# Making the last block's cross keys, first values, first norm and first queries inside its self-attention, and running both cross stages' value matmuls one step later

## The chip, the cores and the metric

The kernel runs on one core of one Trainium2 chip. A core has a matmul engine (PE, whose weight loads the profile calls PEld), a vector engine (DVE), a scalar engine (ACT), GpSimd (POOL) and DMA queues (SP issues most of them). Each engine takes its instructions in the order in which the program gives them; between engines there are semaphores. The metric is the device time of one execution in microseconds; three runs of the kernel took 4175.94 to 4178.57, median 4177.94.

## The reference, cut to what matters

`x` is 4 sequences of 512 tokens of width 256, `ctx` 4 sequences of 64 tokens of width 192, all float32. Four blocks follow each other: block 0 is cross attention with a feed-forward, block 1 self-attention, cross attention and a gated feed-forward, block 2 four layers of a state-space scan, and block 3:

```python
h = _layernorm(x, ln1_g, ln1_b)
x = x + _mha(h, h, sa_wq, sa_bq, ...)           # 16 heads of 16
h = _layernorm(x, ln2_g, ln2_b)
x = x + _mha(h, context, ca_wq, ca_bq, ...)     # keys and values from ctx
h = _layernorm(x, ln3_g, ln3_b)
h = gelu(h @ mlp_w1.T + mlp_b1) @ mlp_w2.T + mlp_b2
return x + h
```

## The kernel before, in words

A sequence of 512 tokens is four tiles of 128 tokens; there are 16 tiles (NT). `X` holds the residual of all 16 tiles in SBUF.

`layer3` (block 3, line 1784) loads its weights, runs `self_stage`, then `cross_kv`, then `cross_stage`. `layer0` (line 1115 on) runs `cross_kv` and the same `cross_stage`. In both stages the order of the instructions is written out by hand (`tc.manual_schedule()`). Pieces of work are kept in `Pieces`: a piece is a matmul function, an eviction function and a condition. `work(n)` takes the first piece whose condition holds from the queues `front`, `prep`, `fill`, in this order (and at most one from `fill` per call), and issues its matmuls; `evict(n)` issues the evictions of what `work` issued and then n steps of the generator at the head of `norms`. `until(ok)` alternates the two until a condition holds.

`self_stage` (line 849) loops over 64 softmax steps `k` in block 3 (`SPG` = 16 for each of 4 sequences) and four more. A step issues scores (L948, two PSUM tiles of two banks), the maximum nm (DVE, L959), four exponentials (ACT, L963), the transposes of the step before (PE, L977), whose copies pT are made by ACT (L980) and DVE (L982), and the values' matmuls (L996). Between them stand projections of the next sequence (ps_q, ps_k, ps_v; L185 is the helper `matmul_k`), the norm of the next sequence (`norm`, L612 to L622, with rstd on POOL in L616 and a bias added to X on POOL in L1112) and the output projection ps_wo with its eviction into X (L917). All projections share one PSUM buffer, "mi". After the last sequence the four ps_wo stand alone.

`cross_kv` (line 227 on) makes the cross keys and values: two key groups (ps_k), whose eviction kT_c (L249) DVE spreads over the heads with a mask into the block-diagonal Kbd (L250), Vbd zeroed on POOL (L233) and four value groups ps_v, evicted in two halves each (L271).

`cross_stage` (line 654) first makes the norm of sequence 0 (block 3 only), its transposes (`features`, ps_tr, L639, evicted as hT in L646) and two query groups (ps_q, evicted as qT in L678). Its loop then runs over 19 steps i: scores of tile i (L761, one PSUM buffer), nm and pr (DVE, L770, L772), the exponential (ACT, L773), transposes of tile i-2 (L792) with copies on ACT (L793), the sums and reciprocal of tile i (L778, L779), the division on POOL (L781), and at every odd i from 3 on the values' matmuls of the tile pair (i-3)/2 (L801), with a copy AT on ACT (L810). The output projections of that pair (ps_wo, added to X in L708) go to `front`. When a sequence's four tiles are in X, the second norm (xf), its transposes and hF follow, and `half(b)` issues the feed-forward's first half, 8 groups ps_f (GELU in L731), at i = 8 and 12 and twice behind the loop; it waits for its features with `until`. The second half, ps_w (L747, then a DMA to the output), is `fill` work for later steps. In block 0 `side` work of block 2's prefix runs in between.

Of the kernel before, what the change touches and what calls it, by code (L numbers as in the profile page):

```python
# [8 lines left out]
F32 = mybir.dt.float32  # L9
AF = mybir.ActivationFunctionType  # L10
ALU = mybir.AluOpType
AX = mybir.AxisListType
PSUM = bass.MemoryType.PSUM
DRAM = bass.MemoryType.DRAM

P = 128
B = 4
T = 512
# [39 lines left out]
class Pieces:  # L58
# [47 lines left out]
    def until(self, ok):  # L106
        for _ in range(200):
            if ok():
                return
            self.evict()  # L110
            if not ok():
                self.work()
        raise RuntimeError("a piece never comes")
# [11 lines left out]
def kernel(ctx: ExitStack, tc: tile.TileContext, t: dict, out: bass.AP):  # L125
# [15 lines left out]
    def col(name, i=0, n=1):  # L141
        at = _COL[name][0] + i
        return cols[:, at : at + n]
# [507 lines left out]

        return mm, ev, lambda: b in xns

    def cross_stage(X, pool, psum, Kbd, Vbd, Wq, bq, Wo, W1, b1, W2, ln_q, ln_f, bias_q, bias_f, store=None, side=None, g_tiles=None):

# [7 lines left out]
        if side:  # L665
            side(todo.besides, psum, ("mi", 3))
        at = {"wo": 0, "ff": 0}

        def project(b, c):
            def mm():  # L670
# [12 lines left out]
        def queries(b):  # L683
            if ln_q is None:
                xns[b] = X[:, b * TPB : (b + 1) * TPB, :]
            todo.prep.extend(features(pool, psum, xns, hTs, b, c, ln_q) for c in range(DC))
            todo.prep.extend(project(b, c) for c in range(DC))
# [123 lines left out]
            todo.front.extend(out(g, jj) for jj in range(2))  # L811

        with tc.manual_schedule():
            if ln_q is not None:
                for _ in norm(pool, X, 0, xns, bias_q):
                    pass
            queries(0)
            for i in range(NT + 3):
                b, j = divmod(i, TPB)
                if i < NT and j == 0:  # L820
                    if b >= 2:
                        half(b - 2)
                    if b < B - 1:
                        if ln_q is not None:
                            todo.norms.append(norm(pool, X, b + 1, xns, bias_q))
                        queries(b + 1)
                todo.evict(0)
                if i < NT:
                    scores(i)
                todo.work(2)  # L830
                todo.work_aside()
                todo.go_on(1)
                if 0 <= i - 2 < NT:
                    transposes(i - 2)
                todo.evict(3)
                if i < NT:
                    divided(i)
                todo.work(2, 0)
                if i >= 3 and i % 2 == 1:
                    through_values((i - 3) // 2)  # L840
            for b in (B - 2, B - 1):
                half(b)
            todo.until(lambda: at["ff"] == B)
            while todo.aside or todo.pend:
                todo.work_aside()
                todo.evict(0)
            assert todo.empty()

    def self_stage(X, pool, psum, wide, project, values, Wo, ln, bias, at_end=None, side=None):

# [186 lines left out]
        with tc.manual_schedule():  # L1039
            for _ in norm(pool, X, 0, xns, bias):  # L1040
                pass
            begin(0)
            K = NG * SPG
            lead = 4 if wide else 2
            for k in range(K + 4):
                n, r = divmod(k, SPG)
                if k < K and r == 0:
                    if n < NG - 1:
                        begin(n + 1)
                    elif at_end:  # L1050
                        prep.append((lambda: None, lambda ps: at_end(), None))
                    if n % G == 0 and n // G < B - 1:
                        norms.append(norm(pool, X, n // G + 1, xns, bias, lag=6 if side else 1))
                evict()
                back = k and k <= K
                if back:
                    transposes(k - 1, 0)
                todo.work_aside()
                if k < K:
                    scores(k)  # L1060
                    softmaxed(k)
                if back and k % spc == 0:
                    rs = sums[k // spc - 1]
                    nc.vector.reciprocal(rs, rs)
                if wide:
                    work()
                    evict(0)
                todo.go_on(1)
                through_values(lead // 2)
                evict(0)  # L1070
                if k % 2 or not todo.busy:
                    todo.go_on(1)
                todo.work_aside()
                work()
                evict()
                if back:
                    transposes(k - 1, 1)
                todo.go_on(1)
                todo.work_aside()
                through_values(lead // 2)  # L1080
                evict(0)
                work()
                if back and (wide or (k - 1) % 2 == 1):
                    c, r1 = divmod(k - 1, spc)
                    hc = 2 * c + combos(k - 1)[0][0] // 2
                    pv.extend((hc, t4) for t4 in range(TPB))
            until(lambda: at["wo"] == NG)
            while todo.side or todo.aside or todo.pend:
                todo.work_aside()
                evict()  # L1090
                todo.go_on(1)
            assert todo.empty() and not pv
# [688 lines left out]
                assert not active and len(banks) == 2  # L1781


    def layer3(X, wa):
        with ExitStack() as st:
            wp = st.enter_context(tc.tile_pool(name="w3", bufs=1))
            Wcq = load_w(wp, "L3_cq", [P, DC, D])
            Wck = load_w(wp, "L3_ck", [CP, 2, D], CP)
            Wcv = load_w(wp, "L3_cv", [CP, 2, D], CP)
            Wco = load_w(wp, "L3_co", [P, DC, D])  # L1790
            W1 = load_w(wp, "L3_w1", [P, DC, FF])
            W2 = load_w(wp, "L3_w2", [P, FF // P, D])
            bv, bo, cbv, cbo, mb2 = (row(wp, n) for n in ("l3_bv", "l3_bo", "l3_cbv", "l3_cbo", "l3_mb2"))
            with tc.tile_pool(name="a3s", bufs=1) as pool, tc.tile_pool(name="ps3s", bufs=1, space=PSUM) as psum:

                V2 = [pool.tile([P, TPB, T], F32, name=f"V{i}") for i in range(2)]
                for v in V2:
                    nc.gpsimd.memset(v, 0.0)

                def project(ps, k, m, hT, to=None):  # L1800
                    if hT is not None:
                        matmul_k(ps, [(wa["qk"[k]][:, c, m * P : (m + 1) * P], hT[:, c, :]) for c in range(DC)])
                    elif k == 0:
                        nc.vector.tensor_scalar(to, ps, col("l3_bq", m), 0.25, ALU.add, ALU.mult)
                    else:
                        nc.vector.tensor_scalar(to, ps, col("l3_bk", m), None, ALU.add)  # L1806

                def values(ps, n, j, hT, V=None):
                    if hT is not None:
                        matmul_k(ps[:, :D], [(hT[:, c, j * P : (j + 1) * P], wa["v"][:, c, :]) for c in range(DC)])  # L1810
                        return None
                    V = V2[n % 2]
                    nc.vector.tensor_add(
                        V.rearrange("p c (h r) -> p c h r", r=32)[:, j, :, :16],
                        ps[:, :D].rearrange("p (h r) -> p h r", r=16),
                        bv.rearrange("p (h r) -> p h r", r=16),
                    )
                    return V

                self_stage(X, pool, psum, False, project, values, wa["o"], ("l3_g1", "l3_b1"), bo)  # L1820
            with tc.tile_pool(name="a3c", bufs=1) as pool:
                with tc.tile_pool(name="ps3k", bufs=2, space=PSUM) as psum:
                    Kbd, Vbd = cross_kv(pool, psum, Wck, Wcv, 16, "l3_cbk", cbv)

                def store(i, x):
                    nc.sync.dma_start(out=out[i // TPB, (i % TPB) * P : (i % TPB + 1) * P, :], in_=x)

                with tc.tile_pool(name="ps3c", bufs=1, space=PSUM) as psum:
                    cross_stage(
                        X, pool, psum, Kbd, Vbd, Wcq, "l3_cbq", Wco, W1, "l3_mb1", W2,  # L1830
                        ("l3_g2", "l3_b2"), ("l3_g3", "l3_b3"), cbo, mb2, store,
                    )

    hT_pool = ctx.enter_context(tc.tile_pool(name="hT_pool", bufs=1))
# [46 lines left out]
    with ExitStack() as st:  # L1881
# [13 lines left out]
                nc.sync.dma_start(out=wa[n], in_=t[f"L3_{n}"].rearrange("(c p) n -> p c n", p=P))  # L1895

        layer2(hT, A, far[:, 0:1], h63, tail, X, fw, wl, late)
        layer3(X, wa)


# [68 lines left out]
```

## Time and profile before

| | |
|---|---|
| three runs | 4175.94 to 4178.57 us, median 4177.94 |
| the profiled execution | 4180.51 us, its span 4178.4 us, mean granted clock 0.905 |
| busy share of the span | PE 84%, DVE 72%, POOL 57%, ACT 53% |
| block 0's cross stage, first scores to last ps_w | 26.3 to 277 us |
| block 3's self-attention, last softmax step's nm to last ps_wo | 3899.2 to 3919.5 us |
| block 3's cross keys and values, norm and queries | 3919.5 to 3941 us |
| block 3's first cross scores to the last ps_w | 3941.1 to 4175.4 us |

The profile is one execution. "Busy" is the time in which an engine executes; behind a row of a timeline or of the groups stands in brackets how long the engine sat idle ahead of it and who released it. In a timeline a row is a run of equal instructions: start, length, engine, line, operation, tiles, number. Each float32 matmul of the program shows as two instructions (x8 is four matmuls). The granted clock is a share of PE's full clock.

### The profile page before, as it was taken

What the parts mean: (1) busy time and instruction counts of PE and PEld (TensorE: products, weight loads), DVE (VectorE), ACT (ScalarE), POOL (GpSimd) and SP (SyncE); (2) the same over time, 40 slices, a digit from 0 to 9 for tenths busy, and PEclk for the clock granted to TensorE, in tenths of its full rate; (3) what the DMA queues carried; (4) which work ended last, traced back from release to release, by engine and by line L of the source; (5) the groups of instructions that cost most, each with busy time, mean ns of one, the idle gap of its engine ahead of it and who ended that gap; (6) DMA issues with size and microseconds to landing.
All of it is one profiled execution on the core that took longest, in us unless ns stands there. A gap on an engine that the chain in (4) does not pass through costs nothing. (4 is left out here: it accounts for less than half of the span.)

```text
span 4178.4 us, 48642 instructions
## 1 busy us (share of the span) xinstructions
PE 3494.9 (84%) x17616; PEld 2186.1 (52%) x17616; DVE 3000.8 (72%) x2857; ACT 2195.9 (53%) x4457; POOL 2364.5 (57%) x1601
## 2 busy tenths in 40 slices
PE   7988988988888898788877787888877667999789
PEld 4654544544566464555555555555555444555446
DVE  5537456465555633999999999999999996666653
ACT  2345465454312434666666666666666553566322
POOL 2239259077100413989888988999988881000131
PEclk9999999999988997888888888888888778999899
DMA  2023023033100202444444444444443441000000
GB/s 75 5 86 104 27 74 98 18 91 97 44 1 1 66 18 83 160 152 158 149 162 145 157 154 160 153 153 147 161 157 132 147 144 36 1 1 1 1 6 16
DMA packets 140287, 369.93 MB, mean 89 GB/s; under 512 B 20624, under 2 KB 38224, under 8 KB 140048
## 3 DMA queue, kind: packets, MB, share of 16 engines
q1 hardware_dynamic: 136688, 363.58, 25.6%
q10 hardware_dynamic: 3360, 3.25, 0.3%
q8 instruction: 139, 2.28, 0.2%
q14 instruction: 100, 0.82, 0.1%
HBM read 363.50 MB, written 3.28 MB: 88 GB/s over the span
## 5 line engine op out<-in xcount | busy, mean ns | idle before, releaser
L1617 POOL TENSOR_TENSOR dBu<-dtx,bB 128x1022 f32<-128x1022 f32 x512 | 1198.7, 2361 | 49.1 <-DVE ps_dA L1644 36.8
L1644 DVE TENSOR_TENSOR_SCAN ps_dA<-ps_dA,dBu 128x1024 f32<-128x1024 f32 x384 | 877.9, 2286 | 129.6 <-POOL dBu L1617 88.8
L1629 ACT ACTIVATE ps_dA<-dt,A 128x512 f32<-128x512 f32 x1024 | 708.3, 692 | 469.9 <-DVE hC L1651 426.3
L1677 PE MATMUL ps_y<-ident,hC 128*128 128x128 f32 x3072 | 460.0, 303 | 51.3 <-DVE hC L1651 51.1
L1651 DVE TENSOR_TENSOR hC<-ps_dA,bC 128x1024 f32<-128x1024 f32 x384 | 469.8, 1223 | 23.9 <-issue 0.4
L1677 PEld LDWEIGHTS ps_y<-ident,hC 128*128 128x128 f32 x3072 | 406.8, 158 | 149.5 <-DVE hC L1651 75.6
L963 ACT ACTIVATE pr<-ps_s,nm 128x512 f32<-128x512 f32 x512 | 345.2, 686 | 257.5 <-DVE nm L959 257.5
L959 DVE TENSOR_REDUCE nm<-ps_s 128x2 f32<-128x1024 f32 x256 | 301.5, 1219 | 173.2 <-PE ps_s L948 156.4
L1655 POOL TENSOR_TENSOR hP<-hP,bC 128x1024 f32<-128x1024 f32 x128 | 301.9, 2358 | 108.4 <-issue 36.2
L977 PE MATMUL ps_pt<-ident,pr 128*128 128x128 f32 x2048 | 285.2, 279 | 65.3 <-DVE pT L982 39.5
L977 PEld LDWEIGHTS ps_pt<-ident,pr 128*128 128x128 f32 x2048 | 232.7, 142 | 164.5 <-issue 65.1
L1644 DVE TENSOR_TENSOR_SCAN hP<-ps_dA,dBu 128x1024 f32<-128x1024 f32 x128 | 291.7, 2279 | 0.0
L616 POOL TENSOR_TENSOR ln_rstd<-ln_rstd,const 128x4 f32<-128x4 f32 x24 | 24.4, 1018 | 462.2 <-DVE ln_rstd L615 461.9
L535 DVE TENSOR_TENSOR_SCAN phb<-pdA,phb 128x512 f32<-128x512 f32 x128 | 228.7, 1799 | 73.7 <-POOL phb L525 50.3
L178 PE MATMUL ps_cv<-xp,w_dg 128*128 128x512 f32 x512 | 241.9, 607 | 32.0 <-ACT xp L1427 16.3
L996 PE MATMUL ps_o<-pT,V 128*64 128x256 f32 (+1 forms) x2048 | 220.2, 391 | 1.8 <-ACT AT L1014 1.8
L1677 PE MATMUL ps_y<-ident,hP 128*128 128x128 f32 x1024 | 156.1, 303 | 73.6 <-POOL hP L1655 73.6
L982 DVE COPY pT<-ps_pt 128x512 f32<-128x512 f32 x256 | 164.8, 680 | 63.6 <-PE ps_pt L977 63.1
L948 PE MATMUL ps_s<-kT,qT 64*128 64x512 f32 (+1 forms) x1024 | 206.5, 641 | 1.5 <-DVE kT L1806 0.8
L525 POOL TENSOR_TENSOR phb<-hT_res,pm 128x512 f32<-128x512 f32 x128 | 189.1, 1482 | 29.2 <-DMA pm<-scrp 21.2
L980 ACT COPY pT<-ps_pt 128x512 f32<-128x512 f32 x256 | 139.9, 594 | 118.8 <-PE ps_pt L977 118.5
L1677 PEld LDWEIGHTS ps_y<-ident,hP 128*128 128x128 f32 x1024 | 133.4, 157 | 106.3 <-POOL hP L1655 81.1
(272 smaller groups left out, 6250.1 us busy)
## 6 DMA issues: line engine op xcount, KB each, us to landing
bB<-scr SPq DMA_DIRECT2D x256, 512.0 KB, 4.1
bC<-scr SPq DMA_DIRECT2D x256, 512.0 KB, 3.7
pm<-scrp SPq DMA_DIRECT2D x224, 256.0 KB, 3.1
w_pw_in<-in_L_in SPq DMA_DIRECT2D x7, 512.0 KB, 4.6
X<-in_x SPq DMA_DIRECT2D x4, 512.0 KB, 7.6
w_L_W<-in_L_W SPq DMA_DIRECT2D x2, 1024.0 KB, 10.0
w_L_Wq<-in_L_Wq SPq DMA_DIRECT2D x2, 1024.0 KB, 4.9
w_L_Wo<-in_L_Wo SPq DMA_DIRECT2D x2, 1024.0 KB, 9.2
```

The lines of the kernel that those rows point to most:

```text
L178: nc.tensor.matmul(dst, l, r, start=(i == 0), stop=(i == len(pairs) - 1))
L535: nc.vector.tensor_tensor_scan(hb, dA, hb, 0.0, ALU.mult, ALU.add)
L959: nc.vector.tensor_reduce(nm, ps, AX.X, ALU.max, negate=True)
L963: nc.scalar.activation(pr, ps[:, x, :], AF.Exp, bias=nm[:, x : x + 1], accum_out=rs[:, y : y + 1])
L977: nc.tensor.transpose(pp[:, t4, :], pr[:, t4 * P : (t4 + 1) * P], ident)
L996: nc.tensor.matmul(ps_o[0][j * stride : (j + 1) * stride, half * W2 : (half + 1) * W2], Vs[n][0][:, t4, h * stride : (h + 1) * stride], pT ...
L1617: nc.gpsimd.tensor_mul(dBu[:, :, 1:], dtx[:, 1:].unsqueeze(1).broadcast_to([P, 2, T - 1]), bmap[i // 2, 0][:, :, 1:])
L1629: nc.scalar.activation(dA, dt, AF.Exp, scale=A[:, l, m, s : s + 1])
L1644: nc.vector.tensor_tensor_scan(to, dA, dBus.pop(i).rearrange("p s t -> p (s t)"), 0.0, ALU.mult, ALU.add)
L1651: nc.vector.tensor_mul(hCs[i], dA, bmap[i // 2, 1])
L1655: nc.gpsimd.tensor_mul(hCs[i], hCs[i], bmap[i // 2, 1])
L1677: nc.tensor.matmul(y[:, j, k * P : (k + 1) * P], hC[:, s, j * P : (j + 1) * P], ident, is_transpose=True, start=False, stop=(2 * s2 + s == ...
```

## The change: what it does

1. In `layer3` the cross keys, the first sequence's cross values, the first cross norm and the first cross queries are issued inside `self_stage`. Two keys and one value become `fill` pieces from step k = K - SPG on (PSUM buffer "mi"); the spreading of the keys moves from DVE (2 products of 128x2048) to POOL (8 of 128x512) as a generator in `norms`, with the norm of X's sequence 0 behind it; kT_c has one buffer. Behind the last softmax step `tail` issues the transposes and the queries between the last ps_wo, in PSUM buffers "pt".
2. Kbd now lies in hT_res, which block 2 has left, Vbd and the first qT in tiles of block 2's weight pool. Vbd's memset stands before the hand-ordered part; in the built program it comes in POOL's stream near the end of block 2.
3. `cross_stage` takes the ready queries (`begun`) and starts with the scores; the values of sequences 1 to 3 are `fill` pieces of its first steps.
4. In both cross stages the loop has 20 steps, and the values' matmuls of pair (i-4)/2 come at even i from 4 on.

```diff
-            if ln_q is not None:
-                for _ in norm(pool, X, 0, xns, bias_q):
-                    pass
-            queries(0)
-            for i in range(NT + 3):
+            if not begun:
+                if ln_q is not None:
+                    for _ in norm(pool, X, 0, xns, bias_q):
+                        pass
+                queries(0)
+            for i in range(NT + 4):
...
-                if i >= 3 and i % 2 == 1:
-                    through_values((i - 3) // 2)
+                if i >= 4 and i % 2 == 0:
+                    through_values((i - 4) // 2)
...
+                if fill and k == K - SPG:
+                    todo.fill.extend(fill(psum))
                 if k < K and r == 0:
                     if n < NG - 1:
                         begin(n + 1)
-                    elif at_end:
+                    else:
+                        if follows:
+                            norms.append(follows)
+                    if n == NG - 1 and at_end:
...
+            if tail:
+
+                more = tail(psum)
+                todo.evict(0)
+                while at["wo"] < NG or more:
+                    work()
+                    if more and (more[0][2] is None or more[0][2]()):
+                        mm, ev, _ = more.pop(0)
+                        todo.pend.append((ev, mm()))
+                    evict(0)
...
+                def blocks():
+
+                    mask = col("mask", 0, 8).unsqueeze(2).broadcast_to([P, 8, S])
+                    for m in range(DC):
+                        while m not in kTs:
+                            yield
+                        for b in range(B):
+                            nc.gpsimd.tensor_mul(
+                                Kbd[:, m, b], kTs[m][:, b, :].unsqueeze(1).broadcast_to([P, 8, S]), mask
+                            )
+                            yield
+                        spread.add(m)
+                    yield from norm(pool, X, 0, xns, cbo)
...
+                def contexts(psum):
+                    return [key(psum, 0), value(psum, 0), key(psum, 1)]
+
+                def tail(psum):
+                    return [
+                        features(pool, psum, xns, hTs, 0, c, ("l3_g2", "l3_b2")) for c in range(DC)
+                    ] + [query(psum, c) for c in range(DC)]
...
+                    follows=blocks(), tail=tail, fill=contexts,
...
-                    Kbd, Vbd = cross_kv(pool, psum, Wck, Wcv, 16, "l3_cbk", cbv)
...
+                        begun=qT0, fill=[value(psum, b, 3) for b in range(1, B)],
```

`key`, `value` and `query` are pieces with the matmuls and evictions that `cross_kv` and `project` have.

More of the change, by code (lines that the diff above doesn't have):

```diff
@@ L652, in features, with cross_stage @@
         return mm, ev, lambda: b in xns
-    def cross_stage(X, pool, psum, Kbd, Vbd, Wq, bq, Wo, W1, b1, W2, ln_q, ln_f, bias_q, bias_f, store=None, side=None, g_tiles=None):
+    def cross_stage(X, pool, psum, Kbd, Vbd, Wq, bq, Wo, W1, b1, W2, ln_q, ln_f, bias_q, bias_f, store=None, side=None, g_tiles=None, begun=None, fill=()):
         xns, hTs, xf, hF, qTs, pTs, ATs, outs, gTs = {}, {}, {}, {}, {}, {}, {}, {}, {}
@@ L667, in cross_stage @@
         at = {"wo": 0, "ff": 0}
+        if begun:
+            qTs[0] = begun
+        todo.fill.extend(fill)
         def project(b, c):
@@ L847, in cross_stage, with self_stage @@
             assert todo.empty()
-    def self_stage(X, pool, psum, wide, project, values, Wo, ln, bias, at_end=None, side=None):
+    def self_stage(X, pool, psum, wide, project, values, Wo, ln, bias, at_end=None, side=None, follows=None, tail=None, fill=None):
         G = 2 if wide else 1
@@ L1781, in layer2, with layer3 @@
                 assert not active and len(banks) == 2
-    def layer3(X, wa):
+    def layer3(X, wa, wl):
         with ExitStack() as st:
@@ L1818, in values @@
                     return V
-                self_stage(X, pool, psum, False, project, values, wa["o"], ("l3_g1", "l3_b1"), bo)
+                Kbd = hT.rearrange("p c b t -> p (c b t)").rearrange("p (m b h s) -> p m b h s", m=DC, b=B, h=8)
+                Vbd = wl.tile([P, B, H // 2, 2, 16], F32, name="Vbd", tag="inz")
+                q0 = wl.tile([P, DC, T], F32, name="qT0", tag="out")
+                nc.gpsimd.memset(Vbd, 0.0)
+                kTs, xns, hTs, qT0, spread = {}, {}, {}, [None, 0], set()
@@ new lines, in key, with mm, ev @@
+                def key(psum, m):
+                    def mm():
+                        ps = psum.tile([P, T], F32, name="ps_k", tag="mi", bufs=1)
+                        matmul_k(ps[:, : B * S], [(Wck[:, c, m * P : (m + 1) * P], ctxT[:, c, :, 0, :]) for c in range(2)])
+                        return ps
+                    def ev(ps):
+                        kT = pool.tile([P, B, S], F32, name="kT_c", tag="kT_c", bufs=1)
+                        nc.vector.tensor_scalar(kT.rearrange("p b s -> p (b s)"), ps[:, : B * S], col("l3_cbk", m), None, ALU.add)
+                        kTs[m] = kT
+                    return mm, ev, lambda: m == 0 or m - 1 in spread
@@ new lines, in value, with mm, ev @@
+                def value(psum, b, bufs=1):
+                    def mm():
+                        ps = psum.tile([P, T], F32, name="ps_v", tag="mi", bufs=bufs)
+                        matmul_k(ps[:, :D], [(ctxT[:, c, b].rearrange("p r s -> p (r s)"), Wcv[:, c, :]) for c in range(2)])
+                        return ps
+                    def ev(ps):
+                        psv = ps[:, :D].rearrange("p (h r d) -> p h r d", r=2, d=16)
+                        bvv = cbv.rearrange("p (h r d) -> p h r d", r=2, d=16)
+                        for r in range(2):
+                            q = slice(r * 64, (r + 1) * 64)
+                            nc.vector.tensor_add(Vbd[q, b, :, r, :], psv[q, :, r, :], bvv[q, :, r, :])
+                    return mm, ev, None
@@ new lines, in query, with mm, ev @@
+                def query(psum, c):
+                    def mm():
+                        ps = psum.tile([P, T], F32, name="ps_q", tag="pt", bufs=2)
+                        matmul_k(ps, [(Wcq[:, k, c * P : (c + 1) * P], hTs[0, 0][:, k, :]) for k in range(DC)])
+                        return ps
+                    def ev(ps):
+                        qT0[0] = q0
+                        nc.vector.tensor_scalar(qT0[0][:, c, :], ps, col("l3_cbq", c), 0.25, ALU.add, ALU.mult)
+                        qT0[1] = c + 1
+                    return mm, ev, lambda: (0, 1) in hTs
@@ new lines, in contexts @@
+                def contexts(psum):
[4 more added lines that the diff above has]
+                    ] + [query(psum, c) for c in range(DC)]
+                self_stage(
+                    X, pool, psum, False, project, values, wa["o"], ("l3_g1", "l3_b1"), bo,
+                    follows=blocks(), tail=tail, fill=contexts,
+                )
@@ L1821, in layer3 @@
             with tc.tile_pool(name="a3c", bufs=1) as pool:
-                with tc.tile_pool(name="ps3k", bufs=2, space=PSUM) as psum:
-                    Kbd, Vbd = cross_kv(pool, psum, Wck, Wcv, 16, "l3_cbk", cbv)
                 def store(i, x):
@@ L1897 @@
         layer2(hT, A, far[:, 0:1], h63, tail, X, fw, wl, late)
-        layer3(X, wa)
+        layer3(X, wa, wl)
 def _layout(a):
```

## The prediction

> **What bounds the kernel now.** I read the page's slices, the table by windows around the stage the change touches, the chain that ended last, and the timelines of PE and DVE. The profiled execution took 4180.51 us, its span 4178.4; the median of the three runs is 4177.94, so I add the change to the profiled time and then take off 2.6. From 3450 on only the last block runs, PE is busy 83 to 93% of most windows, and the chain of waits there is almost all PE. One stretch differs (columns: window, its length, busy us and instructions of PE, PEld, DVE, ACT, POOL, granted clock, DMA):
>
> ```profile
> 3915.00:3920.00 5.00, 3.85 (x16) 2.74 (x16) 0.88 (x3) 0.00 (x0) 0.45 (x1) 1.00 0.00 0
> 3920.00:3925.00 5.00, 3.69 (x16) 2.96 (x16) 4.93 (x12) 0.00 (x0) 0.51 (x1) 1.00 0.00 0
> 3925.00:3930.00 5.00, 2.43 (x6) 2.01 (x7) 3.74 (x8) 0.00 (x0) 1.02 (x1) 0.58 0.00 0
> 3930.00:3935.00 5.00, 2.63 (x10) 1.85 (x9) 3.64 (x11) 0.00 (x0) 2.96 (x4) 0.50 0.00 0
> 3935.00:3940.00 5.00, 4.95 (x9) 2.14 (x9) 2.86 (x7) 0.00 (x0) 0.00 (x0) 0.56 0.00 0
> ```
>
> PE is half idle, then half clocked. The chain shows why: after the self-attention's last projection (ps_wo) comes the cross keys' and values' work on DVE (the chain calls it issue, POOL waiting), then the first norm, the transposes, the queries, and only then the first scores:
>
> ```profile
> 3917.45 2.01 PE ps_wo L185 x8
> 3919.55 0.95 POOL Vbd L233
> 3920.51 8.00 issue
> 3928.55 1.03 POOL ln_rstd L616
> 3929.60 2.19 DVE xn L622 x4
> ...
> 3935.69 5.53 PE ps_q L185 x8
> 3941.22 1.98 PE ps_s L761 x4
> 3943.23 1.24 DVE nm L770
> ```
>
> In both cross stages the values' matmuls (L801) stand on PE right behind transposes whose copies ACT makes only after the next exponential, and the scores behind them then run slowly:
>
> ```profile
> 81.85 1.57 PE L801 MATMUL ps_o<-pT,Vbd 128*32 128x256 f32 x16 [4.29 <-ACT pT L793]
> ...
> 3966.56 1.84 PE L801 MATMUL ps_o<-pT,Vbd 128*32 128x256 f32 x16 [3.35 <-ACT pT L793]
> 3968.33 2.86 PE L761 MATMUL ps_s<-Kbd,qT 128*128 128x512 f32 x4
> ...
> 3981.43 1.94 PE L801 MATMUL ps_o<-pT,Vbd 128*32 128x256 f32 x16 [4.74 <-ACT pT L793]
> 3983.29 3.78 PE L761 MATMUL ps_s<-Kbd,qT 128*128 128x512 f32 x4
> ```
>
> The eight waits in block 3 add up to 11 us of idle PE (3.35, 4.74, 0.24, 0.65, 0.24, 0.24, 1.29, 0.24), those of block 0 to about 10.
>
> **Term 1, the transition: -16.2.** Before, from the first of the four ps_wo (3909.71) to the first nm (3943.23) is 33.5 us. In the changed order PE has ps_wo, ps_wo, ps_wo, a transpose group, ps_wo, the other group, four query matmuls, scores. A ps_wo starts every 2.57 us while only its eviction (0.42, gap 0.59) separates it: three end at 7.15. A transpose group lasts 0.9 to 1.0 at full clock and covers the third gap: 8.1. Then ps_wo 2.0 (10.1), the group 0.9 (11.0), the queries 3.6 (the ps_q row at 4046) with a short wait for the second hT: 14.6. The scores wait for the second qT (0.75): 15.5, take 1.7, and nm follows: 17.3. 33.5 - 17.3 = 16.2 saved. I take full clock: PE has no gap above 0.6 there, and the windows with such ps_wo show 1.00. The page "TensorE: Matmul & The Clock Gate" of the Trainium skill (section "What's actually happening") says the array halves its clock after an idle window of about 3.4 us and needs as long a busy one to return; the 3.81 us gap before the values at 3927.57 and the 0.50 to 0.58 behind it agree, the scores at 44.68 (3.64 us after a gap of 2.14) do not quite. If the queries ran as slowly as before (5.5), the saving would be 14.3: that is the bound on this side; with no gap between the ps_wo, 17.5 on the other.
>
> **Term 2, what the last sequence now carries: +3.0.** Two keys and one value on PE, their evictions, four norm statistics and four xn on DVE stand in sequence 3's softmax steps, whose ring (scores, nm, exponential, transposes, copies) has no slack for what stands ahead of the pT copies. Sequences 0 to 2 show the price, since they carry the same norm for their successor: a plain step is 5.43 to 5.52 from nm to nm, a step with a statistic on both sides of the copies 6.07:
>
> ```profile
> 3700.29 2.36 DVE L959 TENSOR_REDUCE nm<-ps_s 128x2 f32<-128x1024 f32 x2
> 3702.57 1.28 DVE L982 COPY pT<-ps_pt 128x512 f32<-128x512 f32 x2
> 3703.76 0.41 DVE L612 BATCH_NORM_STATS2 ln_st<-X 128x6 f32<-128x256 f32 x1
> ...
> 3705.72 2.35 DVE L959 TENSOR_REDUCE nm<-ps_s 128x2 f32<-128x1024 f32 x2 [1.33 <-PE ps_s L948]
> ...
> 3711.79 1.23 DVE L959 TENSOR_REDUCE nm<-ps_s 128x2 f32<-128x1024 f32 x1 [1.33 <-PE ps_s L948]
> ```
>
> The step with one statistic behind the copies (3700.29 to 3705.72) cost nothing, the next one 0.6, one with two xn 0.3. Five such steps: 0.6 + 0.6 + 0.2 + 0.3 + 0.3 = 2.0. A step with two small value projections is 6.08 (+0.6), so key, value and key cost 1.0. Bounds: 0, and 8 steps at the 7.80 of a step with two projections, +19. I take the nearer rows. The key's spreading becomes eight GpSimd products (1.04 each by L781's row, 8.3 in all) on an engine that is 0.00 busy from 3880 to 3915; keys are due 50 us later. If that cover went, the scores would wait up to 8.3.
>
> **Term 3, block 3's cross stage: +2.3.** With the values a step later their copies are long done, so the waits go. What is late next? Steps from nm to nm before: 6.05, 6.79, 6.31, 8.85, 6.08, 9.80, 7.21, then 13.43 to the first ps_f. After, by DVE's order: nm and pr 2.48, rs with reciprocal 1.47 (which cannot start before 3.75, the exponential), and what stands between. Step 0: two Vbd (0.58), three statistics (1.74), 6.3. Step 1: Vbd, a statistic, rstd with its GpSimd trip (1.35), xn, 7.0. Step 2: Vbd, three xn (1.46), rs, hT (1.44), PE idle till xn, 8.0. Step 3: 5.8. Step 4: 5.8. Step 5: two X, statistic, rstd, xn: 7.3. Step 6: PE has the values behind the transposes, which wait for three xn, idle some 4.5 us and then slow: 9.3. Then 13.4. Sum 62.9 against 64.5: -1.6. The large waits went, but DVE needs 6 to 7 us a step anyway. In the second half PE is the bound either way. Between the first and second ps_f block 41.5 us grow by 1.0: the last two adds of ps_w now stand ahead of rstd on DVE, so PE idles 5 us before ps_f where it idled 3.2 (and starts colder, +1.0). From the second ps_f to the end PE carries one values-and-projection pair more (1.1 + 1.8), less the waits gone: +1.9. Bounds: -15 (all waits of 11 gone, and 4.4 of slow matmuls behind them), +14 (two ps_f blocks each a step of 7 later). Taken: the worked step sums.
>
> **Term 4, block 0's cross stage: -3.5.** Same edit, with the prefix's side work beside. Steps 4 to 7 end 4.0 earlier (the 4.29 wait and ps_wo's 3.78 behind it go), the first ps_f starts colder (+1.5), the second block comes as before (its norm now waits for three ps_w adds, 3.3 idle, against gaps of 5.6 that shrink), the wait of 2.54 at 195.22 goes against one pair moved (-1.0). Bounds -14 and +7. What block 1 does follows block 0 by the same amount; PE's order there differs only in where the side pieces stand.
>
> **Term 5, the memset: +0.5.** Vbd's memset (0.95) moves from 3919.55 into the end of block 2's GpSimd stream, which is 90% busy. It waits for the matmuls of w_inz, the last at 3369, 80 us before. 0 to 0.95.
>
> Sum: -16.2 + 3.0 + 2.3 - 3.5 + 0.5 = **-13.9**, on the profiled 4180.5 gives 4166.6, by the median 4164. The scale of the profile is such that 0.2% (8.4 us) is about what a measurement here can tell from no change.
>
> **Rivals.**
> - The values' delay pays fully: both stages lose their ACT waits and the slow matmuls behind them, -12 and -8 in place of +2.3 and -3.5, so 4146. For it: the waits are plain PE idle. Against: DVE's 6 to 7 us a step. 0.15.
> - The delay is paid back: norms, transposes and ps_f are late in each half, PE waits there, and the two cross stages together lose 7: 4172, within 0.2%. For it: the idle of 2.27 and 1.6 us before ps_f at 4004 and 4061 is such a wait already. 0.17.
> - Slower: each ps_f block starts a whole step later because its features come a step later and PE has nothing else. Place: the eight ps_f blocks of the two stages; price 7 us each. From three blocks on it eats the 13 and 8 more; with five (+35, -16.2 + 3.5): 4200. Against: in the last two blocks of each stage PE has ps_w matmuls to fill. 0.04.
> - The change does not do what it says: ps_wo would still stand ahead of all of the tail, and the transition saves only the key, value and norm work, about 12 of the 16.2: 4168. Its chance lies within the first.
>
> **How the numbers follow.** The forecast (0.64) has 4155 to 4169: terms 3 and 4 each some 5 off. The range must reach to the rivals until no more than 0.2 is left out: 4152 to 4173. Faster by over 0.2% means below 4169.6: forecast and first rival, 0.79; within 0.2%, the second and a little more, 0.17; slower 0.04.
>
> **What would show it.** Right: from the first ps_wo after the last self-attention values to the first cross nm about 17 us, clock 1.00 there; sequence 3's steps of 5.4 grown to about 6 in eight places; no wait for ACT's pT above 1 us at the values; new DVE waits ahead of ps_f. Wrong: if the queries run at half clock, if a scores matmul waits for GpSimd or for PSUM of the earlier stage, if block 1 starts later than before, or if the last ps_w block does not end about 13 us earlier.

## The result, and the profile after

The changed kernel takes 4156.26 us (median of four runs, 4153.25 to 4157.58) against 4178.12 for the kernel before: -21.9, ratio 0.9946 (95% interval 0.9932 to 0.9960). Its profiled execution took 4156.58 us, span 4154.8, mean granted clock 0.908. The forecast was 4164.0, -13.9: right in sign and inside the range, but the gain is 1.6 times the forecast, and the forecast lies outside the interval (-16.7 to -28.4).

Where the difference of the two spans (-23.6) lies, read from the start of the first maximum (nm, DVE) of each stage to the next mark:

| stretch | before | after | difference | forecast |
|---|---|---|---|---|
| block 0: first cross nm to block 1's first nm | 257.96 | 255.15 | -2.8 | -3.5 (term 4) |
| **block 1's self-attention: first to last nm** | 777.12 | 767.26 | **-9.9** | 0 |
| from there to the first nm of block 3 | 2427.50 | 2426.73 | -0.8 | +0.5 (term 5) |
| block 3's self-attention, last 16 steps' start to the first ps_wo | 97.22 | 99.94 | +2.7 | +3.0 (term 2) |
| transition: first ps_wo to first cross nm | 33.52 | 16.64 | -16.9 | -16.2 (term 1) |
| block 3's cross stage: first nm to the end | 235.17 | 238.17 | +3.0 | +2.3 (term 3) |

Rows left out, the start of the program (+0.25) and the first 48 steps of block 3 (+0.75), add 1.0. Without block 1's self-attention the difference is -13.7, against a forecast of -13.9. That the two agree to 0.2 is luck in part: the cross stages alone scatter by 2 to 3 us between kernels in which their order is the same (below).

The transition, by windows of the changed kernel (columns as before the change: length, busy us and instructions of PE, PEld, DVE, ACT, POOL, granted clock, DMA):

```profile
3900.00:3905.00 5.00, 3.98 (x16) 2.87 (x16) 0.85 (x2) 0.00 (x0) 0.00 (x0) 1.00 0.00 0
3905.00:3910.00 5.00, 4.91 (x25) 4.15 (x26) 1.66 (x4) 0.00 (x0) 0.00 (x0) 1.00 0.00 0
3910.00:3915.00 5.00, 4.02 (x9) 1.36 (x8) 2.31 (x3) 0.00 (x0) 0.00 (x0) 1.00 0.00 0
```

and by the chain that ended last:

```profile
3907.53 1.99 PE ps_wo L185 x8
3909.52 0.44 PE ps_tr L639 x4
3909.95 0.86 PE ps_q L185 x2
3910.86 2.86 PE ps_q L185 x6
3913.74 0.76 DVE qT L1896
```

The 8 us of "issue" and the norm are gone from the chain, the clock column stays at 1.00, and the four query matmuls take 3.7 where they took 5.5. The order is the one that term 1 counted.

In block 3's cross stage the values' matmuls (now L804) no longer wait for ACT's copies; the wait has moved to what stands in their old place (a timeline of PE; idle time ahead of a row in brackets):

```profile
3944.75 1.07 PE L804 MATMUL ps_o<-pT,Vbd 128*32 128x256 f32 x16
...
3960.24 1.97 PE L639 MATMUL ps_tr<-ident,xn 128*128 128x128 f32 x8 [5.44 <-ACT pT L796]
...
3975.82 0.70 PE L639 MATMUL ps_tr<-ident,xf 128*128 128x128 f32 x2 [3.84 <-DVE xf L622]
```

And in block 0, where the wait of 4.29 at 81.85 was, PE now comes to the features of the feed-forward before the second norm has made them, and waits 7.39. The first ps_f group still starts 2.2 sooner after the first nm (59.4 against 61.6):

```profile
85.92 2.20 PE L639 MATMUL ps_tr<-ident,out 128*128 128x128 f32 x8 [7.39 <-DVE out L622]
```

**The unforeseen 9.9 us.** Of the softmax steps of block 1 (from one nm to the next) most are the same to a few hundredths; steps 15 to 19 (of 0 to 63) took 67.1 us and take 58.8, and step 19 alone fell from 19.89 to 15.27. There ACT in the kernel before does this (timeline of ACT):

```profile
526.36 0.22 ACT L963 ACTIVATION_READ_ACCUMULATOR pr<-ps_s,nm 128x1 f32 x1
526.58 1.28 ACT L467 ACT_TABLE_LOAD   x1
527.87 2.00 ACT L467 ACTIVATE hT_res<-hT_res 128x1024 f32<-128x1024 f32 x2
```

and PE this:

```profile
528.98 3.18 PE L185 MATMUL ps_side<-hT_res,w_pw_xp 128*48 128x256 f32 x8 [2.77 <-ACT hT_res L467]
532.09 2.38 PE L185 MATMUL ps_v<-w_L_Wv,hT 128*128 128x512 f32 x4
```

L467 is the SiLU of block 2's prefix (layer 1), side work. It stands on ACT behind the four exponentials of step 19, the last of which ends at 526.58, and PE's next side piece needs its result: 2.77 idle, then 1.3 and 0.4 more because that group and the next run slowly (3.18 and 2.38, undisturbed 1.89 and 1.98). In the changed kernel the same two rows of ACT come one stop of the side work earlier, between the exponentials of step 18 and those of step 19:

```profile
506.09 0.21 ACT L967 ACTIVATION_READ_ACCUMULATOR pr<-ps_s,nm 128x1 f32 x1
...
508.51 1.28 ACT L467 ACT_TABLE_LOAD   x1
509.80 2.00 ACT L467 ACTIVATE hT_res<-hT_res 128x1024 f32<-128x1024 f32 x2
...
516.64 0.69 ACT L967 ACTIVATE pr<-ps_s,nm 128x512 f32<-128x512 f32 x1 [0.39 <-DVE nm L963]
```

and PE finds the result ready, with nothing in brackets:

```profile
518.97 1.89 PE L185 MATMUL ps_side<-hT_res,w_pw_xp 128*48 128x256 f32 x8
```

Theory: the side work is a generator that is advanced by one stop at fixed places of the loops (`todo.go_on(1)`), and it goes on from block 0 into block 1. Block 0's loop has 20 steps in place of 19, so it stands one stop further when block 1 begins, and the pieces of layer 1, the next layer, fall elsewhere among the exponentials. The first rival: the later values themselves give the 9.9. The second: the amount of side work that leaves block 1 counts, not its place. For PE the two traces speak against the second at once: from the first nm of block 1 to the last, PE executes 196 side matmul instructions (tile ps_side) in both kernels, and 76 ahead of them in both. Its idle time there falls from 88.3 to 81.2.

### The profile page after: what moved, and what is told of

Same layout as the page of the kernel before. It is cut to its first block, busy times and chain, and to the rows that moved or that the text cites. A ratio compares the mean times of both kernels' runs of the same rounds, so it can differ in the third digit from the quotient of the medians.

```text
span 4154.8 us, 48637 instructions
## 1 busy us (share of the span) xinstructions
PE 3482.7 (84%) x17616; PEld 2183.1 (53%) x17616; DVE 2994.8 (72%) x2855; ACT 2198.2 (53%) x4459; POOL 2372.2 (57%) x1609
## 5 line engine op out<-in xcount | busy, mean ns | idle before, releaser
L967 ACT ACTIVATE pr<-ps_s,nm 128x512 f32<-128x512 f32 x512 | 345.2, 686 | 258.3 <-DVE nm L963 258.2
L178 PE MATMUL ps_cv<-xp,w_dg 128*128 128x512 f32 x512 | 242.1, 607 | 32.0 <-ACT xp L1446 16.2
L784 POOL TENSOR_TENSOR pr<-pr,rs 128x512 f32<-128x512 f32 x64 | 65.4, 1043 | 229.3 <-DVE rs L782 211.1
```

Source lines behind the costliest of these rows:

```text
L178: nc.tensor.matmul(dst, l, r, start=(i == 0), stop=(i == len(pairs) - 1))
L967: nc.scalar.activation(pr, ps[:, x, :], AF.Exp, bias=nm[:, x : x + 1], accum_out=rs[:, y : y + 1])
```

## The experiments

Each was timed beside the kernel before on one chip; groups of four share a chip (medians of the kernel before there: 4175.15, 4175.84, 4177.39). Single executions of one kernel differ there by up to 26 us, so beside the ratio the stage times of the profiled execution are given. Block 1 takes 767.15 to 767.86 in the nine profiles with the 20th step, and 774.48 to 777.12 in the four with neither the step nor an earlier SiLU; the cross stages repeat within some 3 where the order is the same. Microseconds behind a ratio are the ratio applied to 4178.12; plain differences of the medians are up to 3.2 us away from them. "Steps 15-19" and "block 1" are sums of softmax steps, "block 0" and "block 3" the cross stages as in the table above.

| kernel | ratio to before (95%) | block 0 | block 1 | steps 15-19 | block 3 |
|---|---|---|---|---|---|
| before | | 257.96 | 777.12 | 67.13 | 235.17 |
| after | 0.9946 (0.9932-0.9960) | 255.15 | 767.26 | 58.83 | 238.17 |
| before + 20th step in block 0 | 0.9966 (0.9954-0.9977) | 256.11 | 767.15 | 58.83 | 236.22 |
| before + later values in block 0 | 0.9968 (0.9955-0.9981) | 253.86 | 767.16 | 58.82 | 235.15 |
| after, 19 steps in block 0 | 0.9984 (0.9974-0.9994) | 259.46 | 776.24 | 67.13 | 239.39 |
| after, block 0 as before | 0.9973 (0.9961-0.9985) | 258.20 | 776.73 | 65.47 | 237.19 |
| after again | 0.9948 (0.9933-0.9963) | 255.07 | 767.61 | 58.83 | 238.18 |
| after, old values in block 3 | 0.9949 (0.9933-0.9965) | 253.99 | 767.86 | 58.83 | 235.78 |
| after, old values in both | 0.9960 (0.9945-0.9974) | 258.20 | 774.48 | 65.49 | 236.87 |
| before, SiLU one stop sooner | 0.9985 (0.9974-0.9996) | 255.48 | 771.27 | 61.13 | 236.39 |
| after, 21 steps in block 0 | 0.9945 (0.9933-0.9958) | 253.85 | 767.17 | 58.82 | 238.22 |
| after, first pairs late in block 3 | 0.9946 (0.9933-0.9958) | 255.18 | 767.37 | 58.82 | 237.60 |
| after, tail behind the ps_wo | 0.9940 (0.9928-0.9953) | 254.83 | 767.77 | 58.83 | 237.30 |
| move + 20th step, old values | 0.9947 (0.9934-0.9961) | 254.94 | 767.39 | 58.82 | 237.19 |

**1. The 20th step alone, in the kernel before.**

```diff
-            for i in range(NT + 3):
+            for i in range(NT + (4 if side else 3)):
...
-                if i >= 3 and i % 2 == 1:
+                if 3 <= i < NT + 3 and i % 2 == 1:
```

> The kernel before with one change: the loop of block 0's cross stage has 20 steps instead of 19; the last step only takes side work and pieces, the values' matmuls stay where they were. Theory (phase of the side work): block 1 gained 9 us in the changed kernel because the generator of block 2's prefix stands one step further when block 1's softmax steps begin; then this alone gives -9 and the kernel comes at about 4169. Rival (the delayed values themselves): the step alone gives nothing, 4178, within 2 either way.

Ratio 0.9966, -14.2; block 1 has -10.0, with steps 15 to 19 to the hundredth those of the changed kernel. The step alone does it: the rival with no gain falls. That the whole shows more than 9 is not clear of the noise (the interval is -9.6 to -19.2).

**2. The later values (with the step) in block 0 of the kernel before.**

```diff
+            lag = 4 if side else 3
-            for i in range(NT + 3):
+            for i in range(NT + lag):
...
-                if i >= 3 and i % 2 == 1:
-                    through_values((i - 3) // 2)
+                if i >= lag and i % 2 == lag % 2:
+                    through_values((i - lag) // 2)
```

> The kernel before with the values' matmuls one step later (and 20 steps) in block 0's cross stage only; block 3 as before. If the changed kernel's gain in blocks 0 and 1 comes from this edit, whichever half of it: -2.6 in block 0 and -9 in block 1, about 4166. If block 1's gain came from elsewhere (another placement of tiles, chance): only block 0's -2.6, about 4175.5.

Ratio 0.9968, -13.4, block 1 -10.0. Beside experiment 1 the later values add nothing that these times can tell.

**3. The changed kernel without the step.**

```diff
-            for i in range(NT + 4):
+            for i in range(NT + (3 if side else 4)):
```

> The changed kernel with 19 loop steps instead of 20 in block 0's cross stage; the values stay one step later. Phase theory: the 9 us of block 1 are lost again, block 0's 2.6 stay: about 4165. Rival (the values): nothing is lost, about 4156.

Only -6.7 is left (0.9984), where I expected -13: block 1 is back at 776.2 and 67.1. So the first rival is out. Block 0 loses as well, which I had not expected: 259.46. It loses from the last cross nm to block 1's first nm (102.6; before 96.6, after 97.2): without the step the last pair's output projections come behind the third ps_f block, and PE waits 3.19 and 0.76 for the last features, where the changed kernel does not wait.

**4. The changed kernel with block 0 as before** (lag 3 and 19 steps where there is side work, as in experiment 2 reversed).

> The changed kernel with block 0's cross stage as before (values at odd steps, 19 steps); block 3 as changed. If the edit in block 0 is worth -2.6 and -9: about 4168. If block 1's gain does not hang on it: 4159.

Ratio 0.9973, -11.3, block 1 776.73: block 1's gain hangs on block 0's loop. Steps 15 to 19 take 65.47 and not 67.13, though the order and the wait (2.76) are those of the kernel before: the side group behind the wait took 1.93 here, not 3.18 (more in the last section).

**5. The place of the SiLU by itself, block 0 untouched.** In the kernel before one stop of the generator is left out, in layer 1 between the two convolutions of its first pair of input groups:

```diff
-                    if i == 0:
+                    if i == 0 and (l, m0) != (1, 0):
                         yield
```

> The kernel before with one stop fewer in the prefix's generator, in layer 1 between the two convolutions of the first pair of input groups (no computation is left out; the side work behind that stop comes one side step sooner). Theory: block 1's gain is where the SiLU of layer 1 (with its table load) stands on ACT against the exponentials of softmax step 19; one step sooner it stands ahead of them, step 19 falls from 19.9 to about 15.3, and the kernel gains 4.6, with up to 3.7 more if steps 15 and 17 follow. Rival: the gain needs the extra step in block 0 (an amount of side work moved out of block 1): then this changes nothing.

Ratio 0.9985, -6.3; block 1 -5.9. Step 19 takes 15.28, step 17 7.84 in place of 9.37, step 15 stays 11.08. ACT:

```profile
513.68 1.28 ACT L467 ACT_TABLE_LOAD   x1
514.98 2.00 ACT L467 ACTIVATE hT_res<-hT_res 128x1024 f32<-128x1024 f32 x2
```

and on PE the side piece without a wait:

```profile
524.14 1.89 PE L185 MATMUL ps_side<-hT_res,w_pw_xp 128*48 128x256 f32 x8
```

Block 0's loop is untouched and no side work has moved into it; the gain is the place of the pieces, and the second rival does not explain these 6 us. (Against the other three profiles without the step, 774.48 to 776.73, it is 3 to 5.)

**6. Yet another step of block 0's loop** (`NT + (5 if side else 4)`, values as in the changed kernel).

> The changed kernel with 21 loop steps in block 0's cross stage: the prefix's generator is one more side step ahead when block 1 begins. Phase theory (what counts is where the SiLU and the layer boundary fall among the exponentials): step 19 stays at about 15.3, single steps change by 1 to 2 us in either direction, and the whole stays within 4 of the changed kernel. Rival (amount: each side step moved out of block 1 saves its cost there): another 8 us less, about 4146.

Block 1 767.17, the ratio that of the changed kernel: no further 8 us. In the code the generator waits at a side piece until PE has done it, and by step 13 the extra stop is absorbed: in steps 13 to 19 the side matmuls stand in the same steps as in the changed kernel, and from step 15 to step 26 the steps are the same within 0.04.

**7. The changed kernel once more.**

> The changed kernel itself once more, beside the others on one chip. All theories: 21.9 under the kernel before (ratio 0.9946), steps 15 to 19 of block 1's softmax 58.8 us in sum as in its first profile.

Ratio 0.9948, 58.83: as before.

**8. Old values in block 3 only**, and **9. in both stages** (19 steps): only the move is left in 9.

> The changed kernel with block 3's cross stage taking the values at odd steps again (19 steps); keys, first values, norm and queries stay moved, the values of sequences 1 to 3 stay pieces of the first steps. Theory: in block 3 the later values cost 2 to 3 us (the profiles show +2.85 for this stage, first nm to the end), so this is 2 to 3 under the changed kernel. Rival: the +2.85 come from the value pieces that now stand in the stage's first steps, and the later values save; then it is slower than the changed kernel by some 3 to 6, since the ACT waits of 3.35 and 4.74 are back.

> The changed kernel with both cross stages' values at odd steps and 19 steps: only the move of the keys, values, norm and queries is left. From the profiles: transition -17.1, last self-attention sequence +2.7, so -14.4, and 0 to +3 for the value pieces in block 3's first steps: between 11 and 14.5 under the kernel before; block 1's softmax steps as before (steps 15 to 19: 67.1 us). If block 1's gain hung on something else in the change, it would show -23 here.

In 8 the stage falls by 2.4 in the profile, but the ratio (0.9949) can't be told from that of the changed kernel beside it (0.9948), so no gain is shown; nor is the loss of 3 to 6 that its rival had. In 9 the ratio is 0.9960, -16.7, more than the 11 to 14.5 expected, though its interval (-10.9 to -23.0) holds these. Block 1 has 65.5 in steps 15 to 19, not the 67.1 expected: the wait in step 19 is there (2.76), and the group behind it again takes 1.93. Block 3's stage by kernels: with the order of before 235.2 to 236.4 (four, mean 235.7); with the value pieces and old values 235.8 to 237.2 (three, 236.6); with late values 237.2 to 239.4 (six, 238.1). So by the means the pieces cost about 0.9 and the delay 1.5; single profiles of neighbouring groups overlap or touch.

**10. Late only where ACT's waits were large.**

```diff
+            at_step = [2 * g + (4 if side or g < 3 else 3) for g in range(NT // 2)]
...
-                if i >= 4 and i % 2 == 0:
-                    through_values((i - 4) // 2)
+                if i in at_step:
+                    through_values(at_step.index(i))
```

> The changed kernel, in block 3's cross stage with the values one step later only for the first three pairs (where the profile of the kernel before has the ACT waits of 3.35 and 4.74), and at the old odd steps from the fourth pair on. Theory: the later values cost 1.9 there (first nm to the end: 3.0 with all late, 1.1 with all old) because each sequence's last pair, and with it the second norm and the features, comes a step later; with the last pairs back and the first ones late the stage comes at 0 or below, 3 under the changed kernel. Rival: the first pairs' delay is what costs (DVE's order there); then it stays at about 3.

My theory fell: the stage takes 237.6, not 235 or below, and lies nearer to the rival (+2.4 on the kernel before, where the rival had about 3). Ahead of the second norm's features three ps_w pieces (10.5 us) now run where there were two (7.1), so the second ps_f block starts as late as in the changed kernel (42.7 us after the ninth nm; changed kernel 42.1, before 39.5). Which pair's delay costs the 1.5 is open.

**11. The tail behind the output projections.**

```diff
-                    if more and (more[0][2] is None or more[0][2]()):
+                    if more and at["wo"] == NG and (more[0][2] is None or more[0][2]()):
```

> The changed kernel with the four last output projections ahead of both transposes and the queries (nothing interleaved). By the prediction's counting of the interleaved order (a transpose group covers one gap between output projections): the transition from the first output projection to the first cross nm grows by 1 to 1.5, from 16.4 to about 17.6. Rival (the order of the tail is what the transition gains): it grows by 4.

The transition takes 17.50 in place of 16.64: +0.9, a little under the 1 to 1.5 expected. The interleaving is worth about one gap between projections; the rival with 4 falls. The whole (0.9940) can't be told from the changed kernel.

**12. The move and the 20th step, no later values.**

```diff
-            for i in range(NT + 4):
+            for i in range(NT + (4 if side else 3)):
...
-                if i >= 4 and i % 2 == 0:
-                    through_values((i - 4) // 2)
+                if 3 <= i < NT + 3 and i % 2 == 1:
+                    through_values((i - 3) // 2)
```

> The changed kernel with the values at odd steps in both cross stages, but with the 20th loop step kept in block 0: the move of keys, values, norm and queries, and the extra side step, without any later values. Theory: block 1 gains its 8 to 9 us all the same, block 0 has -1 in place of -2.6, block 3 has +1.1 in place of +3.0: as fast as the changed kernel, within 3. Rival (the later values carry part of block 1's gain): 5 or more slower than the changed kernel.

Ratio 0.9947: the gain of the changed kernel, without the later values. No version that is faster than the changed kernel, beyond the intervals, came out of these runs.

## Why the prediction was right, and where it failed

- **The step that failed** is the last sentence of term 4: "What block 1 does follows block 0 by the same amount; PE's order there differs only in where the side pieces stand". Where the side pieces stand was worth 9.9 us in the first two profiles and 8.7 between the means of all with and without the step, and it comes from the 20th loop step (experiments 1, 3). 8.3 of the 9.9 lie in steps 15 to 19. About 6 come through the place of layer 1's side pieces behind its first convolution, its SiLU above all (experiment 5). The other 4 come with the step too, and no experiment took them apart; in the traces 2.3 of them are step 15, whose side piece stands in step 13 in the changed kernel, where PE was idle before (steps 12 and 13 together: idle 3.44, now 1.35; lengths 27.95 and 27.87). The stall was in the trace of before, as the 2.77 us of PE and the longest softmax step of block 1; I read only the stages whose code the diff touches.
- **Term 1** (-16.2): -16.9, 16.64 or 16.65 in all nine profiles with the move and its interleaved tail. Its mechanism held in order, clock and interleaving.
- **Term 2** (+3.0): +2.7, and 2.7 to 3.6 over the ten profiles with the move. The steps came near the prices: those with statistics on both sides of the copies take 5.96 and 6.07 (the rows below), the step with the first key and the value 6.08, that with the second key 5.88, two with xn 5.75. The sign "about 6 in eight places" was too many: four steps are near 6.

```profile
3843.95 2.35 DVE L963 TENSOR_REDUCE nm<-ps_s 128x2 f32<-128x1024 f32 x2
...
3849.91 2.35 DVE L963 TENSOR_REDUCE nm<-ps_s 128x2 f32<-128x1024 f32 x2 [1.33 <-PE ps_s L952]
...
3855.98 2.36 DVE L963 TENSOR_REDUCE nm<-ps_s 128x2 f32<-128x1024 f32 x2 [1.33 <-PE ps_s L952]
```

- **Term 3** (+2.3): +3.0 in the profile, +2.4 between the means of the runs. To the first ps_f the worked steps came almost one by one (forecast 6.3, 7.0, 8.0, 5.8, 5.8, 7.3, 9.3, 13.4; measured 6.19, 6.83, 8.30, 6.03, 5.42, 6.72, 9.87, 12.91): -2.2, forecast -1.6. Behind it two parts were mis-sized, and one the other way: from the end of the first ps_f block to the second +2.5 (forecast +1.0), the second block itself 16.29 where it took 14.00 (+2.3, forecast +1.0), from its end on +1.0 (forecast +1.9). The first block was 0.7 shorter, which had no term. The near sum is luck in part.
- **Term 4 in block 0** (-3.5): -2.8. The size is near, but it is no larger than the scatter of profiles with the order of before (255.5 to 258.2), and the reason held only in part: the step alone brings block 0 to 256.1 and 254.9, the later values together with the step to 253.9 to 255.2, and the later values without the step to 259.5. The 4.29 us wait went, but the 7.39 at 85.92 came; up to the first ps_f 2.2 is left of the gain.
- **Term 5** (+0.5): nothing of it can be seen; the stretch from block 1 to block 3 scatters by more.
- **Rivals.** "The values' delay pays fully" gave 4146 and lies on the side to which the time went, but its mechanism did not happen: with old values the time is the same (experiment 12). "Paid back" has its direction in block 3 alone (+3.0, block 0 -2.8): the two stages together lost 0.2, not 7. The slower rival needed each ps_f block a whole step later; in block 3 the first came earlier (62.3 us after the first nm, before 64.5), and the second too by this count (121.1, before 121.5), though 2.6 later counted from the ninth nm. That the change doesn't interleave is shown wrong by the chain.

## What to carry to other kernels

Where side work is advanced by counting calls, an edit that adds or takes one call can shift what follows, in stages that the edit does not touch; look there for producers on a second engine that sit just behind its in-order main work and feed a piece that the first engine meets in order. Here such a stall made the longest of a stage's softmax steps, and moving its producer one stop was worth some 5 us by itself. A wait that is removed by issuing the consumer later may come back at whatever stood behind it: here the waits of 3.35, 4.74 and 4.29 went, and 5.44 and 7.39 came at the transposes in or behind their old place.

## What the runs showed of the hardware

- PE's clock fell after an idle of 2.77 us in the kernel before: granted 0.64 in the next window, and the group behind it took 3.18 where it takes 1.89 undisturbed (columns as above).

```profile
526.00:530.00 4.00, 1.23 (x6) 0.62 (x5) 0.00 (x0) 3.86 (x5) 0.00 (x0) 0.94 0.00 0
530.00:534.00 4.00, 4.00 (x10) 1.64 (x9) 0.00 (x0) 0.37 (x1) 0.00 (x0) 0.64 0.03 8
```

  The page "TensorE: Matmul & The Clock Gate" of the Trainium skill (section "What's actually happening") puts the fall behind an idle window of about 3.4 us; here a shorter gap was enough.
- The slow start is not fixed by the gap alone. Of the four profiles with this wait (2.76 or 2.77), the group behind it took 3.18 and 3.16 in the kernel before and in experiment 3, but 1.93 in experiments 4 and 9; this is the difference of 1.65 in their step 19. The row of experiment 4:

```profile
530.72 1.93 PE L185 MATMUL ps_side<-hT_res,w_pw_xp 128*48 128x256 f32 x8 [2.76 <-ACT hT_res L467]
```

  Likewise the same gaps ahead of the second ps_f block of block 3 (0.73, 0.40, 0.47) were followed by 14.00 us in the kernel before and by 15.70 in experiment 8.
- Switching ACT from exponentials to SiLU cost one load of 1.28, with no idle time between the last exponential, the load and the SiLU (rows at 526.36 to 527.87 above). The page "ScalarE: Activation LUTs" of the Trainium skill (section "What ACT_TABLE_LOAD costs") has 1283 ns for the load, which agrees, and about 1380 ns of drain beside it, which these rows do not show.
